# Second expert layer as seven block products with a transposed output

## The chip, the cores and the metric

The kernel runs on one core of a Trainium2 chip. Its engines run side by side, each with a queue of its own that is worked off in order: TensorE (PE; its weight loads are shown as PEld), VectorE (DVE), ScalarE (ACT), GpSimd (POOL) and SyncE (SP), which issues transfers. The metric is device time in microseconds (us) for one execution; the time before is the median of three runs.

## The reference

A block of a transformer on x of 8 x 1024 tokens with 256 numbers each, all in float32. First comes attention with 16 heads, rotary positions and a residual. Then a mixture of 8 experts: each expert takes the 1024 tokens with the highest gate score out of all 8192, and adds its gated output to their rows.

```
xf = layernorm(x).reshape(8192, 256)
scores = softmax(xf @ gate_w.T)             # 8192 x 8 experts
vals, idx = top_k(scores.T, 1024)           # per expert: 1024 tokens
y = layernorm(xf[idx]) * ln_w + ln_b        # 1024 x 256 for each expert
h = gelu(y @ fc1.T + b1)                    # 1024 x 1024
out = (h @ fc2.T + b2) * vals               # 1024 x 256
xf = xf.at[idx].add(out)
```

## The kernel before

The attention stage fills roughly the first 1680 us of the profiled execution. After it, a search by bits finds each expert's threshold, and from about 1747 us on the experts follow one another. The change lies in this expert stage alone.

The work of one expert e has these parts:

- **Token list** (`token_list`, built in pieces by `list_piece`): VectorE compares, TensorE sums small products (L1142) into `ps_i`, and VectorE writes the list `idx` of 1024 rows. It is worked on piece by piece, one or two experts ahead.
- **Gather** (`gather`): eight indirect transfers on GpSimd's queue (L1179), 128 rows each, fetch tokens and gates into two tiles `g`.
- **Turned rows** (`turned_rows`): 8 transposes on TensorE for each half (L1194) and two operations on VectorE (L1195) give `yT`, with the 256 dimensions on the partitions and 512 tokens along the row.
- **First layer**: expert 0 is computed plainly (`first_layer`, L1238). Experts 1 to 7 use a 2x2 block form with 7 block products instead of 8 (`first_layer_by_seven`, L1279): the blocks are the two halves of 256 dimensions, of 1024 hidden units and of 1024 tokens. Sums of weight blocks are made by GpSimd (`weight_sums`, L1257 to L1260), sums of token blocks by VectorE (`row_sums`, L1266 to L1269). For each f of 0 to 3, seven matmuls of 128x512 write seven PSUM banks from the pool `ps_h` (5 banks). ScalarE copies the first product (L1291), VectorE recombines (L1295 to L1324), and ScalarE applies gelu with the bias (L1231), giving `hT`: hidden units on the partitions, tokens along the row.
- **Second layer** (`second_layer`, L1333): for each of 8 tiles of 128 tokens, 8 matmuls of 128x256 with `hT` as the stationary operand give a tile with tokens on the partitions. VectorE adds the bias (L1341) and multiplies by the gate, one number per partition (L1342). GpSimd scatters the tile into `out` with an adding indirect transfer (L1343). These scatters write the same tensor, and each waits until the one before has landed.

The order of all engines' work is the order in which the program is written (`manual_schedule`): nothing is reordered. The loop over experts writes the first layer of e, then its second layer tile by tile, and between the tiles the preparation of expert e+1 (gathers before tiles 0 and 1, `weight_sums` before tile 2, turned rows before tiles 4 and 5) and a piece of list e+2 before each tile. The last expert, 7, splits its first layer in a part "a" before the second layer and a part "b" between its tiles.

Each profiled matmul of the program appears as two records in float32, so a second-layer tile shows 16 records. A transpose appears as one.

## Time and profile before

| | |
|---|---|
| runs before | 2210.72, 2214.38, 2216.36 us; median 2214.38 |
| profiled execution | 2207.54 us, span 2205.8 us |
| busy over the span | PE 93%, DVE 80%, ACT 63%, POOL 58% |
| granted TensorE clock, mean | 0.978 |
| expert 1, first layer, from | 1812.7 us |
| last token scatter issued at | 2200.31 us |

"Busy" is the time in which an engine works on something; an engine can hold its queue without being busy, while its next instruction waits. The tables by line give an operation's count and mean time. Start times count from the start of the span. The chain of waits follows the work that ended last back in time and names the engine whose work it was at each moment.

### The profile page before, as it was taken

Reading aid. Unit: us, or ns where it says so; the run is one execution under the profiler, and the core shown is the slowest. Engines: PE = TensorE matmul, PEld = TensorE weight load, DVE = VectorE, ACT = ScalarE, POOL = GpSimd, SP = SyncE. Lnnn points to the kernel's source line nnn. Section 1 sums busy time; section 2 is a strip of 40 time slices with the busy share of each in tenths; the row PEclk is TensorE's granted clock in tenths of the full one; section 3 lists DMA queues with packets and bytes.
Section 4 is the critical chain, followed back from the end, with each engine's and each line's share of the span. In section 5 each row is a group of like instructions: output and inputs, shape, how many; then the busy total and the mean of one; then the engine's idle time right before and its main releaser. Section 6 shows DMA issues by size and latency. Waiting matters only on the chain.

```text
span 2205.8 us, 35134 instructions
## 1 busy us (share of the span) xinstructions
PE 2056.1 (93%) x12528; PEld 1100.0 (50%) x12528; DVE 1765.4 (80%) x3446; ACT 1384.7 (63%) x1791; POOL 1272.5 (58%) x1320
## 2 busy tenths in 40 slices
PE   7999999999999999999999999999993599999998
PEld 4444544444444444444444444444431376666665
DVE  8988888998998899889989988989946646666654
ACT  2777777777887777878777877877781112222222
POOL 6667585848485766758584867644242144444442
PEclk9999999999999999999999999999996699999999
DMA  6523624632372356236323722552114033333322
GB/s 178 191 88 123 238 81 147 223 122 78 136 257 73 104 202 206 96 107 225 143 78 143 270 67 102 188 208 88 41 41 135 20 75 75 77 77 77 76 42 24
DMA packets 152703, 271.53 MB, mean 123 GB/s; under 512 B 15056, under 2 KB 67664, under 8 KB 152400
## 3 DMA queue, kind: packets, MB, share of 16 engines
q1 hardware_dynamic: 139088, 250.62, 32.9%
q0 software_dynamic: 12288, 17.05, 4.7%
q8 instruction: 99, 1.62, 0.3%
q10 hardware_dynamic: 1152, 1.62, 0.2%
q14 instruction: 76, 0.62, 0.1%
HBM read 143.93 MB, written 125.04 MB: 122 GB/s over the span
## 4 chain that ended last, share of the span: by engine, by line
PE 71%; DVE 16%; issue 4%; POOL 3%; ACT 2%; DMA 2%; POOLq 0%; ACTq 0%; SPq 0%; DVEq 0%
PE ps_av L639 20%; DVE mx L543 14%; PE ps_x L536 13%; PE ps_o L1333 10%; PE ps L1279 8%; PE ps_s L587 7%; PE ps_p L292 5%; PE ps_t L251 3%; PE ps_o L727 3%; PE ps_h L1238 1%; POOL xf L242 1%; ACT e L620 1%; PE ps_d L665 1%; DVE xr L735 1%; PE ps_y L1194 1%
## 5 line engine op out<-in xcount | busy, mean ns | idle before, releaser
L543 DVE TENSOR_REDUCE mx<-ps_x 128x1 f32<-128x512 f32 x2048 | 1264.1, 681 | 153.1 <-PE ps_x L536 139.8
L620 ACT ACTIVATE e<-ps_s 128x1024 f32<-128x1024 f32 x1024 | 995.4, 1025 | 88.6 <-PE ps_x L536 42.1
L536 PE MATMUL ps_x<-k,q 64*128 64x512 f32 x2048 | 718.9, 449 | 19.7 <-DVE mx L543 6.2
L587 PE MATMUL ps_s<-q,s 64*128 64x512 f32 x2048 | 622.2, 428 | 9.0 <-ACT e L620 6.1
L536 PEld LDWEIGHTS ps_x<-k,q 64*128 64x128 f32 x2048 | 347.4, 185 | 414.1 <-DVE mx L543 287.8
L639 PE MATMUL ps_av<-e,v 128*32 128x512 f32 x4096 | 492.5, 598 | 6.9 <-DVE mx L543 0.9
L654 POOL TENSOR_TENSOR av<-av,avp 128x512 f32<-128x512 f32 x190 | 242.4, 1276 | 396.4 <-ACT avp L652 380.2
L587 PEld LDWEIGHTS ps_s<-q,s 64*128 64x128 f32 x2048 | 314.0, 185 | 46.9 <-ACT e L620 29.6
L1333 PE MATMUL ps_o<-w,hT 128*128 128x256 f32 x1024 | 230.2, 381 | 0.0
L639 PEld LDWEIGHTS ps_av<-e,v 128*32 128x32 f32 x4096 | 107.0, 109 | 241.7 <-issue 163.6
L1343 POOL DMA_INDIRECT out<-o,idx x64 | 103.0, 1609 | 212.9 <-DVE o L1342 80.2
L1333 PEld LDWEIGHTS ps_o<-w,hT 128*128 128x128 f32 x1024 | 191.8, 190 | 29.3 <-issue 4.8
L652 ACT COPY avp<-ps_av 128x512 f32<-128x512 f32 x192 | 112.8, 587 | 144.4 <-PE ps_av L639 139.9
L1231 ACT ACTIVATE hT<-mid,b 128x512 f32<-128x512 f32 x112 | 77.9, 719 | 98.9 <-DVE mid L1306 73.9
L1291 ACT COPY mid<-ps 128x512 f32<-128x512 f32 x28 | 16.0, 571 | 195.7 <-PE ps L1279 195.7
L292 PE MATMUL ps_p<-wqkv,xnT 128*128 128x512 f32 (+1 forms) x288 | 129.8, 578 | 4.5 <-DVE mx L543 4.1
L1341 DVE TENSOR_TENSOR o<-ps_o,b2b 128x256 f32<-128x256 f32 x64 | 27.1, 423 | 128.8 <-PE ps_o L1333 126.2
L269 POOL TENSOR_TENSOR u<-pe,sin 128x256 f32<-128x256 f32 (+1 forms) x128 | 86.2, 695 | 53.8 <-ACT pe L263 53.8
L1179 POOL DMA_INDIRECT g<-rows_d,idx x64 | 63.9, 998 | 92.1 <-issue 68.0
L339 POOL CAST hi<-full 128x512 fp32r<-128x512 f32 x60 | 36.9, 615 | 89.8 <-ACT full L337 80.7
L273 POOL TENSOR_TENSOR qk<-pe,u 128x512 f32<-128x512 f32 (+1 forms) x72 | 83.3, 1157 | 7.2 <-DVE pe L271 2.2
L340 POOL TENSOR_TENSOR lo<-full,hi 128x512 fp32r<-128x512 f32 x60 | 76.9, 1281 | 7.5 <-DMA s_d<-dlo 2.9
(200 smaller groups left out, 2323.8 us busy)
## 6 DMA issues: line engine op xcount, KB each, us to landing
s<-s_d SPq DMA_DIRECT2D x64, 512.0 KB
k<-k_d SPq DMA_DIRECT2D x62, 512.0 KB
q<-q_d SPq DMA_DIRECT2D x124, 256.0 KB
s_d<-dhi SPq DMA_DIRECT2D x32, 512.0 KB
s_d<-dlo SPq DMA_DIRECT2D x32, 512.0 KB
w<-in_fc_t SPq DMA_DIRECT2D x16, 1024.0 KB
q_d<-hi SPq DMA_DIRECT2D x30, 512.0 KB
q_d<-lo SPq DMA_DIRECT2D x30, 512.0 KB
```

What stands on the lines that cost most here:

```text
L269: eng.tensor_tensor(u[:, :, a * hd : (a + 1) * hd], v4[:, :, 1 - a, :], s3, ALU.mult)
L292: nc.tensor.matmul(pp, lhsT=xnT[:, kc, t % T2 * P : (t % T2 + 1) * P], rhs=w.rearrange("p a d -> p (a d)") if n == DC else w, start=(kc == 0),
L536: nc.tensor.matmul(pt, lhsT=q[r : r + 64, h // 2, j * P : (j + 1) * P], rhs=k[r : r + 64, h // 2, kh * QW : (kh + 1) * QW], start=True, st ...
L543: nc.vector.tensor_reduce(grp[i]["mx"][:, kh, h, j : j + 1], pt, AX.X, ALU.max)
L587: nc.tensor.matmul(pt[:, h % 2, :], lhsT=ones_r[r : r + 64, :] if last else k[r : r + 64, pair, kt * P : (kt + 1) * P], rhs=(top_bufs[half ...
L620: nc.scalar.activation(e.rearrange("p h q -> p (h q)"), pt.rearrange("p h q -> p (h q)"), AF.Exp, scale=DH**-0.5,)
L639: nc.tensor.matmul(pa[HS * h : HS * (h + 1), :], lhsT=v_bufs[b % 2][:, kt, c : c + HS], rhs=es[h // 2][:, h % 2, :], start=(n == 0), stop= ...
L652: nc.scalar.copy(part, pa)
L654: (nc.vector if end else nc.gpsimd).tensor_tensor(av, av, part, ALU.add)
L1279: nc.tensor.matmul(ph, lhsT=lhsT, rhs=rhs, start=True, stop=True)
L1333: nc.tensor.matmul(po, lhsT=h[:, f, j * P : (j + 1) * P], rhs=weights[e][1][:, f, :], start=(n == 0), stop=(n == FC - 1),)
L1343: nc.gpsimd.indirect_dma_start(out=out_rows[:, :], out_offset=bass.IndirectOffsetOnAxis(ap=idx[:, t : t + 1], axis=0), in_=o, in_offset=No ...
```

## The change

For experts 1 to 6 the second layer also becomes a 2x2 block form with 7 block products. The blocks are the two halves of the 256 output dimensions, of the 1024 hidden units and of the 1024 tokens.

- The weights become the stationary operand and the hidden values, 128x512, the moving one. Each product is 4 matmuls of 128x512 into one bank of `ps_h`. The output comes out transposed: dimensions on the partitions, tokens along the row.
- GpSimd makes four sums of second-weight blocks (`second_weight_sums`), written at the start of expert e.
- VectorE makes four sums of hidden blocks for each f (`sum_hidden`), written behind the first layer of f+1. One of them overwrites a block of `hT`.
- VectorE recombines the products; the bias enters with ScalarE's copy of the first product and with one VectorE operation. For this the bias is loaded a second time with output dimensions on the partitions (`b2t`).
- The recombined blocks are turned back by TensorE, 2 transposes for each tile of 128 tokens (`leave`), into the two banks of `ps_o`. ScalarE multiplies by the gate while copying out, and GpSimd scatters as before.
- The first half of the tokens leaves after six products, before the last one. The second half leaves in the next expert, after its first-layer step f=0 (`later`).
- The preparation of e+1 and the list pieces are placed by `between`, called twice in each product (slots 0 to 13). Three slots hold no list piece, so 11 do.
- To make room, `hT` has 2 buffers instead of 3, the buffers `mid2` and `mid3` 2 instead of 4, some list tiles one fewer; `o` has 7 instead of 4.

Experts 0 and 7 keep the second layer as it was, and the attention stage is untouched.

```diff
--- before.py
+++ after.py
@@ -986,6 +986,12 @@
     )
 
 
+    b2t = sel.tile([P, E, 2], F32, name="b2t")
+    with nc.allow_non_contiguous_dma("16 numbers per partition"):
+        nc.scalar.dma_start(b2t, b2.rearrange("e (i p) -> p e i", p=P))
+    nc.gpsimd.tensor_tensor(b2t[:, :, 1], b2t[:, :, 1], b2t[:, :, 0], ALU.subtract)
+
+
     lane_i = sel.tile([P, P], I32, name="lane_i")
     nc.gpsimd.iota(lane_i, pattern=[[1, P]], base=0, channel_multiplier=0)
     lane = sel.tile([P, P], BF16, name="lane")
@@ -1104,7 +1110,7 @@
         n_odd, HIGH, CH = P // LOW, K // LOW, 1024 // LOW
         order = turn if n_odd == 2 else lane[:, 0:HIGH]
         mine = by_token[:, e].rearrange("p b t -> p (b t)")
-        halves_i = hot.tile([P, 2, NT], I32, tag="halves_i", name=f"halves_i{e}")
+        halves_i = hot.tile([P, 2, NT], I32, tag="halves_i", name=f"halves_i{e}", bufs=1)
         nc.vector.tensor_scalar(halves_i[:, 0], mine, LOW - 1, None, ALU.bitwise_and)
         nc.vector.tensor_scalar(halves_i[:, 1], mine, LOW.bit_length() - 1, None, ALU.logical_shift_right)
 
@@ -1124,12 +1130,12 @@
             two = numbers.rearrange("p (l a) -> p l a", a=2).unsqueeze(1)
             return two.to_broadcast([P, tiles, two.shape[2], 2])
 
-        high = hot.tile([P, NT, HIGH], BF16, tag=f"high{LOW}", name=f"high_{e}")
+        high = hot.tile([P, NT, HIGH], BF16, tag=f"high{LOW}", name=f"high_{e}", bufs=3 - n_odd)
         nc.vector.tensor_tensor(
             in_pairs(high), each(split[:, 1], HIGH), rows_of(order, NT), ALU.is_equal
         )
         yield
-        ids = hot.tile([P, NT, 2, HIGH], BF16, tag=f"ids{LOW}", name=f"ids_{e}")
+        ids = hot.tile([P, NT, 2, HIGH], BF16, tag=f"ids{LOW}", name=f"ids_{e}", bufs=3 - n_odd)
         nc.vector.tensor_scalar(ids[:, :, 0, :], high, part, None, ALU.mult)
         nc.vector.tensor_tensor(
             in_pairs(ids[:, :, 1, :]), in_pairs(high), each(lane2, HIGH), ALU.mult
@@ -1151,7 +1157,7 @@
         lows = []
         for c in range(NT // CH):
             yield
-            low = hot.tile([P, 1024], BF16, tag="low", name=f"low_{e}_{c}", bufs=4)
+            low = hot.tile([P, 1024], BF16, tag="low", name=f"low_{e}_{c}", bufs=3)
             low = low.rearrange("p (c l) -> p c l", l=LOW)
             nc.vector.tensor_tensor(
                 in_pairs(low),
@@ -1225,7 +1231,7 @@
             )
 
     def hidden(e, half):
-        return act.tile([P, FC, 512], F32, tag="hT", name=f"hT_{e}_{half}", bufs=3)
+        return act.tile([P, FC, 512], F32, tag="hT", name=f"hT_{e}_{half}", bufs=2)
 
     def activated(e, f, h, src, cols=slice(0, 512)):
         nc.scalar.activation(
@@ -1248,7 +1254,7 @@
 
 
     FH = FC // 2
-    MIDS = {1: 2, 2: FH, 3: FH, 4: 2, 5: 2}
+    MIDS = {1: 2, 2: 2, 3: 2, 4: 2, 5: 2}
 
     def weight_sums(e):
         w = weights[e][0]
@@ -1291,11 +1297,11 @@
             nc.scalar.copy(m1, p1)
             p6 = bank(6)
             product(p6, s[:, 1, lo], t[:, 1])
-            u2 = mid(2)
+            u2 = mid(2) if e + 1 < E else hidden_sum(e, 0)[:, f]
             nc.vector.tensor_tensor(u2, p6, m1, ALU.add)
             p7 = bank(7)
             product(p7, s[:, 2, lo], t[:, 2])
-            u3 = mid(3)
+            u3 = mid(3) if e + 1 < E else hidden_sum(e, 1)[:, f]
             nc.vector.tensor_tensor(u3, p7, u2, ALU.add)
             kept[e, f] = u2, u3
         if "b" in part:
@@ -1324,6 +1330,98 @@
             nc.vector.tensor_tensor(c12, p3, u2, ALU.add)
             activated(e, f, hs[1], c12)
 
+
+
+    def hidden_sum(e, i):
+
+        if (e, i) not in hidden_sums:
+            hidden_sums[e, i] = one.tile([P, FH, 512], F32, tag=f"hsum{i}", name=f"hsum{i}_{e}")
+        return hidden_sums[e, i]
+
+    def sum_hidden(e, f, hs):
+
+        t1, t2, t4 = (hidden_sum(e, i)[:, f] for i in range(3))
+        lo, hi = f, FH + f
+        nc.vector.tensor_tensor(t1, hs[1][:, lo], hs[0][:, lo], ALU.subtract)
+        nc.vector.tensor_tensor(t2, hs[1][:, hi], t1, ALU.subtract)
+        nc.vector.tensor_tensor(t4, hs[0][:, hi], t2, ALU.subtract)
+        nc.vector.tensor_tensor(hs[1][:, lo], hs[1][:, hi], hs[1][:, lo], ALU.subtract)
+
+    def second_weight_sums(e):
+        w = weights[e][1]
+        a = [[w[:, k * FH : (k + 1) * FH, i * P : (i + 1) * P] for k in range(2)] for i in range(2)]
+        s = one.tile([P, 4, FH, P], F32, tag="w2sum", name=f"w2sum_{e}")
+        nc.gpsimd.tensor_tensor(s[:, 0], a[1][0], a[1][1], ALU.add)
+        nc.gpsimd.tensor_tensor(s[:, 1], s[:, 0], a[0][0], ALU.subtract)
+        nc.gpsimd.tensor_tensor(s[:, 2], a[0][0], a[1][0], ALU.subtract)
+        nc.gpsimd.tensor_tensor(s[:, 3], a[0][1], s[:, 1], ALU.subtract)
+        sums2[e] = s
+
+    def second_layer_by_seven(e, hs, between):
+
+
+        w, s = weights[e][1], sums2[e]
+        t1, t2, t4 = (hidden_sum(e, i) for i in range(3))
+        lo, hi = slice(0, FH), slice(FH, FC)
+        mid = lambda i: act.tile([P, 512], F32, tag=f"mid{i}", name=f"mid{i}", bufs=MIDS[i])
+        slot = [0]
+
+        def product(i, a, b):
+            pt = ps_h.tile([P, 512], F32, tag="ph", name=f"ps_{i}")
+            for c in range(FH):
+                if c % 2 == 0:
+                    between(slot[0])
+                    slot[0] += 1
+                nc.tensor.matmul(
+                    pt, lhsT=a[:, c, :], rhs=b[:, c, :], start=(c == 0), stop=(c == FH - 1)
+                )
+            return pt
+
+        def leave(half, parts):
+
+            g = gathered[e, half]
+            for j in range(4):
+                po = ps_o.tile([P, D], F32, tag="po", name="ps_o")
+                for i, part in enumerate(parts):
+                    nc.tensor.transpose(
+                        po[:, i * P : (i + 1) * P], part[:, j * P : (j + 1) * P], ident
+                    )
+                o = act.tile([P, D], F32, tag="o", name="o", bufs=7)
+                nc.scalar.mul(o, po, g[:, j, D + e : D + e + 1])
+                add_to_out(e, 4 * half + j, o)
+
+        p1 = product(1, w[:, lo, 0:P], hs[0][:, lo])
+        m1 = mid(1)
+        nc.scalar.activation(m1, p1, AF.Identity, bias=b2t[:, e, 0:1])
+        p2 = product(2, w[:, hi, 0:P], hs[0][:, hi])
+        c11 = mid(5)
+        nc.vector.tensor_tensor(c11, p2, m1, ALU.add)
+        p6 = product(6, s[:, 1], t2)
+        u2 = mid(2)
+        nc.vector.tensor_tensor(u2, p6, m1, ALU.add)
+        p7 = product(7, s[:, 2], hs[1][:, lo])
+        u3 = mid(3)
+        nc.vector.scalar_tensor_tensor(u3, p7, b2t[:, e, 1:2], u2, ALU.add, ALU.add)
+        p4 = product(4, w[:, hi, P:D], t4)
+        c21 = mid(4)
+        nc.vector.tensor_tensor(c21, p4, u3, ALU.add)
+        p5 = product(5, s[:, 0], t1)
+        nc.vector.tensor_tensor(u2, p5, u2, ALU.add)
+        nc.vector.tensor_tensor(u3, p5, u3, ALU.add)
+        leave(0, (c11, c21))
+        p3 = product(3, s[:, 3], hs[1][:, hi])
+        nc.vector.tensor_tensor(u2, p3, u2, ALU.add)
+        return lambda: leave(1, (u2, u3))
+
+    def add_to_out(e, t, o):
+        nc.gpsimd.indirect_dma_start(
+            out=out_rows[:, :],
+            out_offset=bass.IndirectOffsetOnAxis(ap=lists[e][:, t : t + 1], axis=0),
+            in_=o,
+            in_offset=None,
+            compute_op=ALU.add,
+        )
+
     def second_layer(e, half, j, h):
         idx, t, g = lists[e], 4 * half + j, gathered[e, half]
         po = ps_o.tile([P, D], F32, tag="po", name="ps_o")
@@ -1337,19 +1435,14 @@
                 start=(n == 0),
                 stop=(n == FC - 1),
             )
-        o = act.tile([P, D], F32, tag="o", name="o", bufs=4)
+        o = act.tile([P, D], F32, tag="o", name="o", bufs=7)
         nc.vector.tensor_tensor(o, po, b2b[:, e, :], ALU.add)
         nc.vector.tensor_scalar(o, o, g[:, j, D + e : D + e + 1], None, ALU.mult)
-        nc.gpsimd.indirect_dma_start(
-            out=out_rows[:, :],
-            out_offset=bass.IndirectOffsetOnAxis(ap=idx[:, t : t + 1], axis=0),
-            in_=o,
-            in_offset=None,
-            compute_op=ALU.add,
-        )
+        add_to_out(e, t, o)
 
     assert KT == 8 and FC == 2 * FH
     lists, gathered, turned, sums, row_sum, kept = {}, {}, {}, {}, {}, {}
+    hidden_sums, sums2 = {}, {}
     places(0, 1)
     keep_busy(10)
     for _ in token_list(0, P // 2, 0):
@@ -1402,33 +1495,44 @@
             if half == 1 and j == 3:
                 row_sums(1)
             second_layer(0, half, j, h)
+    later = None
     for e in range(1, E):
         if e + 1 < E:
             load_weights(e + 1)
+            second_weight_sums(e)
         hs = [hidden(e, half) for half in range(2)]
         for f in range(FH):
             first_layer_by_seven(e, f, hs, "ab" if e + 1 < E else "a")
+            if later is not None:
+                later()
+                later = None
             list_piece(1, e + 1)
+            if e + 1 < E and f > 0:
+                sum_hidden(e, f - 1, hs)
         if e + 1 < E:
+            sum_hidden(e, FH - 1, hs)
             list_piece(99, e + 1)
-        for t in range(KT):
-            if e + 1 < E:
-                if t < 2:
-                    gather(e + 1, t)
-                if t == 2:
+
+            def between(i):
+                if i in (0, 2):
+                    gather(e + 1, (i - 0) // 2)
+                if i == 5:
                     weight_sums(e + 1)
-            list_piece(1, e + 2)
-            if e + 1 < E:
-                if t in (4, 5):
-                    turned_rows(e + 1, int(t == 5))
-                if t == 5:
+                if i >= 3:
+                    list_piece(1, e + 2)
+                if i in (9, 11):
+                    turned_rows(e + 1, int(i == 11))
+                if i == 12:
                     row_sums(e + 1)
-            second_layer(e, t // 4, t % 4, hs[t // 4])
-
-
-            if e + 1 == E and t < FH:
-                first_layer_by_seven(e, t, hs, "b")
-
+
+            later = second_layer_by_seven(e, hs, between)
+        else:
+
+
+            for t in range(KT):
+                second_layer(e, t // 4, t % 4, hs[t // 4])
+                if t < FH:
+                    first_layer_by_seven(e, t, hs, "b")
 
 # ---- launch: one core; numpy only lays the arrays out ----
 def _rotary_tables(n, d):
```

## Prediction

> **What bounds the kernel now.** I read the page's slices first, then busy time by stage, then the chain of waits over the expert stage, then the queues of VectorE, ScalarE and GpSimd in order of time. The slices show that TensorE fills the expert stage; by stage, one steady expert (55.6 us) looks like this (columns: window, length, busy PE, PEld, DVE, ACT, POOL, granted clock, DMA share, GB/s):
>
> ```profile
> PE   7999999999999999999999999999993599999998
> 1923.00:1978.60 55.60, 55.60 (x266) 38.16 (x265) 36.82 (x68) 13.11 (x20) 26.40 (x20) 1.00 0.35 77
> ```
>
> PE is busy 55.6 of 55.6 us at clock 1.00. The chain of waits (start, length, work) runs through PE alone: first layer (L1279), second layer (L1333), turned rows (L1194), pieces of token list (L1142). At the very end it leaves PE for the scatters into out:
>
> ```profile
> 1923.02 6.01 PE ps L1279 x14
> 1947.92 10.36 PE ps_o L1333 x48
> 1974.89 0.19 PE ps_i L1142 x8
> 1975.08 3.56 PE ps_o L1333 x16
> 2128.57 0.87 PE ps_y L1194 x8
> 2191.14 3.86 DMA out<-o,idx
> ```
>
> GpSimd is "busy" for 26.4 us only, but its queue stands far longer: each scatter waits until the one before has landed. ScalarE's three activations and VectorE's sums give the other prices:
>
> ```profile
> 2191.14 1.54 POOL L1343 DMA_INDIRECT out<-o,idx  x1 [3.03 <-DMA out<-o,idx]
> 2195.75 1.54 POOL L1343 DMA_INDIRECT out<-o,idx  x1 [3.07 <-DMA out<-o,idx]
> 2200.31 1.54 POOL L1343 DMA_INDIRECT out<-o,idx  x1 [3.02 <-DMA out<-o,idx]
> 1961.01 1.85 POOL L1257 TENSOR_TENSOR wsum<-w 128x512 f32<-128x512 f32 x1
> 1964.72 1.26 POOL L1259 TENSOR_TENSOR wsum<-w 128x512 f32<-128x512 f32 x1
> 1928.47 2.04 ACT L1231 ACTIVATE hT<-mid,b 128x512 f32<-128x512 f32 x3 [0.54 <-DVE mid L1313]
> 1969.45 0.68 DVE L1266 TENSOR_TENSOR ysum<-yT,yT 128x512 f32<-128x512 f32 x1
> 1970.16 0.69 DVE L1267 TENSOR_TENSOR ysum<-yT,ysum 128x512 f32<-128x512 f32 x1
> 1970.77 0.69 DVE L1268 TENSOR_TENSOR ysum<-yT 128x512 f32<-128x512 f32 x1
> ```
>
> Scatters that follow each other stand 4.56 to 4.61 us apart here (4.46 to 4.68 elsewhere). VectorE's operations start 0.71 us apart where one needs the last, 0.60 otherwise.
>
> **Matmuls.** I call F the start of an expert's first layer, S the start of its second, p1 to p7 its products in the order p1, p2, p6, p7, p4, p5, p3. Removed: 8 tiles x 3.455 us (10.36 / 3) = 27.64. Added: 28 matmuls of 128x512; the first layer has the same shape at 6.01 / 7 = 0.858 us, so 24.02. Added: 16 turns of 128x128; eight turned rows take 0.87, so 1.74. A change of work costs the next group 0.10 (3.56 against 3.455), twice: 0.20. Sum 25.96, so PE saves 1.68 us per expert if nothing waits. The list pieces and turned rows are the same number as before.
>
> The Trainium skill ("TensorE: Matmul & The Clock Gate", Part 4: PE-mode transpose) gives about 275 ns for a 128x128 turn inside a kernel, which speaks against this change: 16 would be an estimated 4.4 us and the saving would be a loss of 1.0. The trace's mean for one is 276 ns as well, but eight in a row advance the chain by 0.87, which is what I use.
>
> **New wait 1: turning back the second half.** It is issued after f=0 of the next expert. Two output tiles are free; the third pair of turns waits until ScalarE has scaled the first. In ScalarE's queue that scaling stands behind f=0's four activations, the last of which ends at F+7.49 (1928.47 + 2.04 - 1923.02). The scaling of 128x256 out of PSUM is not in the trace: below it a copy of 128x128 (0.27) and above it an activation of 128x256 (0.47); a copy of 128x512 is 0.59. I take 0.42. So pair three starts at F+7.97, pair four 0.36 later, the pairs take 0.22, and f=1 starts at F+8.55 instead of 6.01 + 0.87: 1.67 us lost (1.4 to 1.9), with all of f=1 queued behind and VectorE idle too. The first half is turned with ScalarE free: the same wait costs 1.37 against 0.87, so 0.50 (0.4 to 0.6).
>
> **VectorE.** Removed per expert: 8 x (0.42 + 0.35) of bias and gate. Added: 16 sums of hidden blocks and 7 recombinations. In the recorded order the list pieces leave the first layer, the hidden sums enter it. For f=1 on (clock from its start): 7 operations need 0.71 x 2 + 0.60 x 5 = 4.42, four sums 0.71 x 2 + 0.60 x 2 = 2.62, together 7.04 against 6.01 on PE. Sums of f=0 run from 6.65, f=2 from 9.27, its sums from 13.69, f=3 from 16.31, the last sums until 25.97, that is S+7.95. Five PSUM banks just cover it: f=3's last product starts at 17.17 and needs a bank that is read by 17.00. Products p1 and p2 cover the sums that p6 needs. But the new list's first piece comes after: 7.95 + 1.07 (four small ones, 1948.57 to 1949.64) + 0.60 + 0.66 + 0.68 = S+10.96, and PE wants it at S+10.3: 0.70 lost (0 to 2.0, since 0.25 us more or less per step moves it by that).
>
> **Sums of second weights on GpSimd.** Four operations, 5.1 to 7.4 us by the rows 1.26 and 1.85. They have one buffer that p3 of the expert before reads last, and four scatters stand ahead, so they run at about S+41 to S+47 of that expert: F+11 to 17 of the next, well ahead of their reader at S+6.9. They hide, but their end lies beside VectorE's first hidden sums. The slow rows 1.85 and 1.81 are those beside VectorE's work on SBUF, so I add 0.5 us of lag per expert (0 to 2.5: four operations held one each).
>
> The skill ("SBUF — State Buffer", Who interferes with whom) says a VectorE operation with two SBUF inputs and a GpSimd one that reads SBUF exclude each other. By that all overlap would be paid, an estimated 1 to 2 us per expert; the rows show only 0.5 to 0.6 per operation.
>
> **GpSimd's queue.** Per period: two runs of four scatters at 3 x 4.57 + 1.54 = 15.25, weight sums 6.2 twice, gathers 8 x 1.27 = 10.2: 53.1 us, under the period. Gathers then start at about S+5.5 rather than S-5, land by S+18.6, and PE turns their second half at S+21.7: hidden, 3 us to spare.
>
> **The end.** For the last changed expert (6; no list pieces) S6 was 2114.76 and the last scatter issued at 2200.31, S6+85.55. Scatters used to leave from S+4 on; now the first waits for six products: 20.6 + 1.82 of turned rows + 0.74 for turn and scaling = S6+23.2. Sixteen scatters then stand in line (8 of this expert, 8 of the last), and those of the last expert would be ready from S6+52, before their turn at 59.8. So the last one issues at 23.2 + 15 x 4.57 = S6+91.75: 6.2 us later (4.5 at 4.46, 7.9 at 4.68). TensorE ends near S6+82, so it no longer matters there.
>
> **At nothing.** Buffers cut from 3 or 4 to 2 or 3: their last readers (p3; a list piece two slots back) are done when they are written. The new load of biases in 4-byte pieces stands last in ScalarE's DMA queue (after 1690.8); behind its wait on GpSimd is the mask that PE reads at 1727.0, a cover of 36 us while the threshold search runs. Such a load is not in the trace; a small one (4 KB) lands in 3.0 us here, and even ten times that is covered; beyond the cover each microsecond would count. Moved weight loads only get earlier.
>
> **Sum.** Per period -1.68 + 1.67 + 0.50 + 0.70 + 0.50 = +1.69. From S1 to S6 there are five periods: +8.45. With the end: +14.65. The profiled execution took 2207.54 (span 2205.8), so 2222.2; the median of the runs is 6.84 above that execution, so I say 2229.
>
> **Rivals.**
> 1. TensorE stays the only limit: faster. No wait costs anything, five periods give -8.4, the end another -1.6: 2204. For it: PE is 100% busy now. Against: the scatters. Even with no stall at all the line of sixteen gives -8.4 + 6.2; a gain above 0.3% (6.6 us, what a measurement here can tell from none) needs spacing below 4.28, and no row has that. 6%.
> 2. Little change (within 6.6 us): PE's waits mostly vanish because scaling is short and VectorE keeps up; -2 to +6, so 2212 to 2221. Against: ScalarE's order fixes wait 1. 16%.
> 3. VectorE and GpSimd become the bound of the first layer: each exclusion is paid and PSUM banks run out, +4 per period, 20 + 6.2: 2241. For it: 7.04 against 6.01, and a bank margin of 0.17. 18%.
> 4. The forecast, waits as summed: 60%.
>
> Low ends together give 5 x 0.12 + 4.5 = +5, high ends 5 x 5.3 + 7.9 = +34, both unlikely. I take 2214 to 2243, into rivals 2 and 3. Faster 0.06, same 0.16, slower 0.78.
>
> **What would show it.** Right: second-layer products at 0.86 us a matmul; a gap on PE of about 1.7 us after f=0, released by ScalarE; a period near 57.3; sixteen scatters in line at the end, about 4.57 apart, with PE done some 10 us before. Wrong: a period at or under 55.6, no PE gap at the turns, or a last scatter released by VectorE's output rather than by the scatter before it.

## The result and the profile after

The changed kernel takes 2237.57 us (median of 4 runs, 2232.74 to 2238.29), the kernel before, run beside it, 2214.93: a ratio of 1.0107, 95% interval 1.0095 to 1.0119. It is slower by 22.6 us. The forecast was 2229, +14.65 in its sum: the right side and mostly the right places, with most of them priced too low and one wait, for PSUM banks, put at nothing.

The profiled execution took 2237.21 us (span 2235.2). 5.40 us of its distance to the one before lie ahead of expert 1 (it starts at 1817.89 instead of 1812.49), 5.20 of them ahead of the threshold search (its first product on PE starts at 1689.54 instead of 1684.34), in work that the change doesn't touch. So I compare the expert stage: from the first product of expert 1 to the issue of the last scatter it was 2200.31 - 1812.49 = 387.82 us, and is 2229.59 - 1817.89 = 411.70, or +23.88, within 1.3 us of the medians.

One steady expert and the page's slice row of PE (columns as in the prediction: window, length, busy PE, PEld, DVE, ACT, POOL, clock, DMA share, GB/s):

```profile
PE   7998999999999999999999999999971899999996
1934.54:1992.47 57.93, 55.08 (x209) 25.81 (x208) 46.64 (x75) 16.99 (x29) 31.96 (x24) 1.00 0.34 73
```

PE was busy for all of its 55.6 us; now it is busy for 55.08 of 57.93. VectorE went from 36.8 to 46.6. Where PE's time goes is seen in its queue in order of time (start, length, line, tile, and in brackets the idle time before with its releaser; `...` stands for rows of work without a gap):

```profile
1940.55 0.60 PE L1386 MATMUL ps_o<-ident,mid 128*128 128x128 f32 x4
1942.61 0.80 PE L1386 MATMUL ps_o<-ident,mid 128*128 128x128 f32 x4 [1.46 <-ACT o L1390]
1943.25 1.02 PE L1285 MATMUL ps<-yT,w 128*128 128x512 f32 x2
...
1960.92 1.13 PE L1285 MATMUL ps<-yT,wsum 128*128 128x512 f32 x2 [0.34 <-DVE mid L1301]
...
1973.16 0.36 PE L1148 MATMUL ps_i<-ids,low 128*128 128x16 bf16 x8 [0.70 <-DVE low L1162]
...
1986.88 0.60 PE L1386 MATMUL ps_o<-ident,mid 128*128 128x128 f32 x4
1987.83 0.80 PE L1386 MATMUL ps_o<-ident,mid 128*128 128x128 f32 x4 [0.35 <-ACT o L1390]
1988.47 0.35 PE L1148 MATMUL ps_i<-ids,low 128*128 128x16 bf16 x8
```

Four stalls. The second half's turns take 2.70 us from start to f=1 (1940.55 to 1943.25) where eight without a wait take 0.87: 1.83 lost, to ScalarE. The last product of f=3 waits for a PSUM bank that VectorE has not read, and S comes 0.61 late by it (1961.89, where 1955.27 and the 6.01 us of an f give 1961.28). The new list comes 0.87 late, from VectorE. The first half's turns take 1.59: 0.72 lost. Together that is 4.03 of the 57.93 us.

ScalarE's queue shows why the first is so long: the scaling (L1390) stands behind three gelus:

```profile
1940.09 2.10 ACT L1237 ACTIVATE hT<-mid,b 128x512 f32<-128x512 f32 x3 [0.41 <-DVE mid L1319]
1942.10 0.82 ACT L1390 ACTIVATE o<-ps_o,g 128x256 f32<-128x256 f32 x2
```

Expert 1 is worse. From the start of its second layer, S1, to that of expert 2, S2, it is 61.55 us; the next three steps are 57.94, 57.92 and 58.84, the last 57.72. VectorE's hidden sums and GpSimd's sums of the next first weights stand beside each other there (queues of VectorE and GpSimd):

```profile
1845.29 1.76 DVE L1345 TENSOR_TENSOR hsum<-hT,hT 128x512 f32<-128x512 f32 x1
1847.08 1.64 DVE L1346 TENSOR_TENSOR hsum<-hT,hsum 128x512 f32<-128x512 f32 x1
1845.23 1.27 POOL L1265 TENSOR_TENSOR wsum<-w 128x512 f32<-128x512 f32 x1
1846.45 1.72 POOL L1266 TENSOR_TENSOR wsum<-w,wsum 128x512 f32<-128x512 f32 x1
```

A hidden sum takes 0.68 to 0.69 where no sum of GpSimd runs beside it. The list then comes 2.58 us late, and after that gap the granted clock falls, so that the next two groups of four records take 3.10 and 2.43 us instead of 1.96 (PE's queue, then the window with the clock in the third column from the end):

```profile
1855.56 0.36 PE L1148 MATMUL ps_i<-ids,low 128*128 128x16 bf16 x8 [2.58 <-DVE low L1162]
1855.77 3.10 PE L1375 MATMUL ps<-hT,w2sum 128*128 128x512 f32 x4
```

```profile
1856.00:1859.00 3.00, 3.00 (x13) 1.06 (x12) 1.30 (x3) 0.00 (x0) 0.00 (x0) 0.58 0.00 0
```

At the end sixteen scatters stand in line, the last ones released by the scatter before (GpSimd's queue). PE is done at 2218.4, 11 us before the last of them is issued:

```profile
2160.01 1.62 POOL L1417 DMA_INDIRECT out<-o,idx  x1 [3.77 <-ACT o L1390]
2166.00 1.57 POOL L1417 DMA_INDIRECT out<-o,idx  x1 [4.37 <-ACT mid L1297]
...
2229.59 1.55 POOL L1417 DMA_INDIRECT out<-o,idx  x1 [3.00 <-DMA out<-o,idx]
```

The first leaves at S6 + 23.64 (S6 is 2136.37), and fifteen gaps of 4.64 on average follow (the first is 5.99, the other fourteen are 4.54 on average).

### The profile page after: what moved, and what is told of

It is laid out like the page before. It is cut to its first block, busy times and chain, and to the rows that moved or that the text cites. A ratio compares the mean times of both kernels' runs of the same rounds, so it can differ in the third digit from the quotient of the medians.

```text
span 2235.2 us, 34636 instructions
## 1 busy us (share of the span) xinstructions
PE 2058.6 (92%) x12192; PEld 1027.6 (46%) x12192; DVE 1829.8 (82%) x3488; ACT 1408.4 (63%) x1845; POOL 1306.6 (58%) x1345
## 5 line engine op out<-in xcount | busy, mean ns | idle before, releaser
L1390 ACT ACTIVATE o<-ps_o,g 128x256 f32<-128x256 f32 x48 | 20.3, 469 | 128.7 <-PE ps_o L1386 128.7
L339 POOL CAST hi<-full 128x512 fp32r<-128x512 f32 x60 | 36.8, 613 | 88.7 <-ACT full L337 81.4
L271 POOL TENSOR_TENSOR pe<-pe,cos 128x512 f32<-128x512 f32 (+1 forms) x64 | 77.5, 1210 | 5.0
L1285 PE MATMUL ps<-ysum,wsum 128*128 128x512 f32 x168 | 77.4, 593 | 0.2 <-DVE mid L1314 0.2
L263 ACT COPY pe<-ps_p 128x512 f32<-128x512 f32 (+1 forms) x64 | 35.9, 561 | 61.9 <-PE ps_p L292 61.9
```

Source lines behind the costliest of these rows:

```text
L1285: nc.tensor.matmul(ph, lhsT=lhsT, rhs=rhs, start=True, stop=True)
```

## The experiments

Each kernel was timed in five rounds against the kernel before. The first column of numbers is the difference to before by medians of one call (the change itself: +22.6), the second the ratio and its interval, the third the expert stage by the trace of one execution, against the 411.70 of the change. The experiments are variants of the changed kernel, and their edits are given against it or against the variant named.

| kernel | us | ratio | stage |
|---|---|---|---|
| k1_banks | +42.9 | 1.0201 (1.0182 to 1.0220) | +12.0 |
| k2_ahead | +15.6 | 1.0075 (1.0059 to 1.0091) | -6.4 |
| k3_wsum | +25.2 | 1.0105 (1.0087 to 1.0124) | +0.5 |
| k4_plain6 | +13.9 | 1.0064 (1.0048 to 1.0079) | -8.5 |
| k6_turnfirst | +23.6 | 1.0113 (1.0097 to 1.0128) | -0.6 |
| k7_nosum | +22.0 | 1.0108 (1.0093 to 1.0123) | -3.6 |
| k8_all | +9.4 | 1.0038 (1.0024 to 1.0052) | -17.6 |
| k9_late | +20.3 | 1.0088 (1.0069 to 1.0108) | -4.1 |
| k10_late_turn | +14.8 | 1.0064 (1.0043 to 1.0085) | -6.6 |
| k11_all | +9.7 | 1.0043 (1.0029 to 1.0058) | -15.8 |
| k12_gather | -1.4 | 0.9994 (0.9985 to 1.0002) | -23.8 |
| k13_apart | -8.8 | 0.9960 (0.9946 to 0.9973) | -32.1 |

The kernel before stands at -23.9 in the last column.

**k1_banks.** Two tiles in each bank of `ps_o`:

```diff
             for j in range(4):
-                po = ps_o.tile([P, D], F32, tag="po", name="ps_o")
+                if j % 2 == 0:
+                    both = ps_o.tile([P, 2, D], F32, tag="po", name="ps_o")
+                po = both[:, j % 2]
```

> The four output tiles that one half turns back share two full PSUM banks (two 128x256 tiles in each), so no turn waits for a scaling of ScalarE. Theory (each period loses what the trace of the changed kernel shows at the turns: 1.84 us in the second half, 0.72 in the first, both released by ScalarE): five periods of 2.56 us give -12.8 us, about 2225; groups of turns advance the chain by 0.87 each, the wait of PE for o is gone, and the first scatter of expert 6 starts some 0.5 us earlier. Rival A (the first layer is held by VectorE and GpSimd anyway, as the prediction's rival 3 has it): VectorE has less time before f=1 and falls behind, the stall comes back as a wait for PSUM banks or for the list, and no more than 1 us per period is won: -5 or less. Rival B: the end's line of scatters sets the time and what PE gains before it is lost there: no change.

A miss: the edit made the wait it was to remove longer, since now each second turn waits for the scaling of the other tile in its bank (PE's queue, steady expert):

```profile
1939.50 0.38 PE L1388 MATMUL ps_o<-ident,mid 128*128 128x128 f32 x2
1941.56 0.66 PE L1388 MATMUL ps_o<-ident,mid 128*128 128x128 f32 x4 [1.68 <-ACT o L1392]
1942.93 0.44 PE L1388 MATMUL ps_o<-ident,mid 128*128 128x128 f32 x2 [0.71 <-ACT o L1392]
```

The turns take 3.70 us instead of 2.70, those of the first half 2.59 instead of 1.59. It still answers something: 2.0 us more of wait made the steady period 1.6 longer (59.5 against 57.9), so a wait at the turns does lie on the path. The later periods are longer still, 60.8 to 61.3. The profiled run was the shortest of five (2245.87 to 2261.86), with a mean granted clock of 0.976; the others lost 9 to 16 us more at 0.969 to 0.972, and where, the trace of this one can't show.

**k2_ahead.** List pieces consumed two pieces later:

```diff
-            yield from token_list(e, P)
+            yield from token_list(e, P, 2)
```

> TensorE consumes each piece of the token list two pieces later instead of one. Theory: PE's wait for the list right after the second layer's first products is 0.9 to 0.95 us in a steady period and 2.6 in expert 1, where the granted clock then falls to 0.58 and costs about 1.9 more; without it 4 x 0.93 + 4.5 = 8 us are won, about 2230, and the clock stays at 1.00 through expert 1. Rival: the list is only where VectorE's lag shows, and its next late result (the mid that p6 or p7 needs) holds PE by as much: no more than 2 us are won.

As the theory had it, with 6.4 of its 8 us. The list wait is gone except for 0.87 us in expert 1, where the clock stays at 1.00; steady periods are 56.8 instead of 57.93.

**k3_wsum and k7_nosum.** The same question, asked twice: first with GpSimd's sums of first weights three slots later, then with the four sums for expert 2 left out, which uses those of expert 1 instead:

```diff
-                if i == 5:
+                if i == 8:
                     weight_sums(e + 1)
```

> The sums of the next expert's first weights on GpSimd are issued three slots later in the second layer (slot 8 instead of 5). Theory: in expert 1 alone they run beside VectorE's last hidden sums (1.76 and 1.64 us instead of 0.68), and moved they leave those at 0.68: VectorE is free some 2 us earlier in expert 1, its list wait shrinks from 2.6 to below 1, the clock does not fall there, and about 3.5 us are won (2234); other experts keep their times within 0.3 us. Rival (the slow hidden sums come from something else, such as the scatter's reads or PE's): the same two sums still take 1.6 us or more and the time is the same within 1 us.

Nothing moved. In GpSimd's queue no other instruction stands between the two slots, so the sums started 0.24 us after the second layer, as before (1846.62 for S1 at 1846.38). The run says nothing on the cause; the second one does:

```diff
-                if i == 5:
+                if i == 5 and e == 1:
+                    sums[2] = sums[1]
+                elif i == 5:
                     weight_sums(e + 1)
```

> Leaves out of the computation the four sums of expert 2's first weights on GpSimd (expert 2 uses those of expert 1); everything else stays. k3_wsum had not moved these sums on GpSimd (nothing stands in its queue between the two slots; they started 0.24 us after the second layer in both). Theory (a VectorE operation on two SBUF operands and a GpSimd one exclude each other): expert 1's two hidden sums of 1.76 and 1.64 us go to 0.68, its list wait shrinks from 2.6 to below 1 us, the granted clock stays at 1.00 there, and 3 to 4 us are won in expert 1 alone, 2234. Rival (they are slow for another reason): no change, within 1 us.

With GpSimd silent, expert 1's last hidden sums take 0.68 and 0.69 (VectorE's queue, the sums that took 1.76 and 1.64), its list wait 0.55 (PE's queue), and the clock is 1.00:

```profile
1843.45 0.68 DVE L1345 TENSOR_TENSOR hsum<-hT,hT 128x512 f32<-128x512 f32 x1
1844.16 0.69 DVE L1346 TENSOR_TENSOR hsum<-hT,hsum 128x512 f32<-128x512 f32 x1
1851.69 0.36 PE L1148 MATMUL ps_i<-ids,low 128*128 128x16 bf16 x8 [0.55 <-DVE low L1162]
```

That is 3.6 us less in the stage, all of it between F1 and F2, the starts of the first layers of experts 1 and 2 (54.88 for 58.57). The medians (-0.6 against the change) are too coarse for it; the trace is the evidence.

**k4_plain6.** Expert 6 with the second layer of the kernel before.

```diff
-            later = second_layer_by_seven(e, hs, between)
+            if e < 6:
+                later = second_layer_by_seven(e, hs, between)
+            else:
+                for t in range(KT):
...
+                    second_layer(e, t // 4, t % 4, hs[t // 4])
```

> Expert 6 alone keeps the plain second layer, with its scatters leaving from the first tile on; experts 1 to 5 are as in the change. Theory (the end is the line of sixteen scatters that starts late): from expert 6's second layer to the last scatter 85.5 us instead of 93.1, that is -7.5 us, about 2230, though TensorE itself does 1.7 us more work there and ends with the scatters. Rival (the end is held by PE's and VectorE's work of the last expert, and the scatters only follow): slower by about 1 to 2 us, since PE has more to do.

Right: 8.5 us in the stage. The last scatters but three are released by VectorE's tile again, 5.17 apart, and only the last three by the scatter before.

**k6_turnfirst.** k1_banks mended: both tiles of a bank are turned, then both are scaled.

```diff
-            for j in range(4):
-                po = ps_o.tile([P, D], F32, tag="po", name="ps_o")
+            for j0 in (0, 2):
+                both = ps_o.tile([P, 2, D], F32, tag="po", name="ps_o")
+                for j in (j0, j0 + 1):
+                    for i, part in enumerate(parts):
+                        nc.tensor.transpose(
...
+                for j in (j0, j0 + 1):
+                    o = act.tile([P, D], F32, tag="o", name="o", bufs=7)
+                    nc.scalar.mul(o, both[:, j - j0], g[:, j, D + e : D + e + 1])
```

> As k1_banks, but both tiles of a bank are turned before either is scaled. k1_banks had each second turn wait for the scaling of its neighbour in the same bank (1.68 and 0.71 us at one half, 0.57 and 0.71 at the other), so that the turns grew by 1.0 us per half instead of shrinking. Theory (a period is as long as what TensorE waits for at the turns, one for one, as long as VectorE is not later than it): now all eight turns of a half follow each other in 0.87 us, 1.84 + 0.72 us per period are won, -12.8 in five, less 0.3 to 0.6 per period if f=3's product waits for a PSUM bank or the list waits longer: -9 to -13, 2225 to 2229. Rival A (VectorE and GpSimd bound the first layer): TensorE's wait only moves to the banks and the list, -5 or less. Rival B (ScalarE's scalings, now later in the queue, hold the next activations and through them the sums): -5 or less, with VectorE's hidden sums waiting for ScalarE's gelus.

The wait that I had counted as the largest is gone, eight turns advance PE by 0.87 (1935.85 to 1936.72), and nothing is won. Rival A holds; rival B doesn't, since VectorE has no gap ahead of its hidden sums and so never waits for a gelu there. PE's waits over the same five periods (engine, line, released by: us in total, times, longest), first of the change, then of k6_turnfirst:

```profile
PE ps_o L1386 <- ACT o L1390: 9.1, 10, 1.5
PE ps_i L1148 <- DVE low L1162: 5.2, 5, 2.6
PE ps L1285 <- DVE mid L1301: 2.1, 6, 0.5
```

```profile
PE ps L1285 <- DVE mid L1301: 10.7, 10, 2.4
PE ps_i L1148 <- DVE low L1162: 5.0, 5, 2.6
PE ps L1285 <- DVE mid L1314: 1.0, 5, 0.2
```

9.1 us of waiting for ScalarE turned into 8.6 more of waiting for VectorE. There are two reasons in VectorE's queue: it needs 7.2 us per f where PE needs 6.0, and because it comes earlier now, its first hidden sums meet GpSimd's sums of second weights. In the change they had come just as the last of these ended (in a steady expert only the first hidden sum was touched, 0.90 for 0.68). The rows are of k6_turnfirst:

```profile
1944.96 1.64 DVE L1346 TENSOR_TENSOR hsum<-hT,hsum 128x512 f32<-128x512 f32 x1
1946.64 1.64 DVE L1347 TENSOR_TENSOR hsum<-hT,hsum 128x512 f32<-128x512 f32 x1
1946.02 1.71 POOL L1357 TENSOR_TENSOR w2sum<-w,w2sum 128x512 f32<-128x512 f32 x1
```

**k8_all.** k6_turnfirst, k2_ahead and k4_plain6 together.

> Turning first (k6_turnfirst), list pieces two ahead (k2_ahead) and a plain second layer for expert 6 (k4_plain6) together. Theory (three separate losses that add up): -10 to -13 for the turns, -8 for the list, -9 for the end, together -27 to -30 against the change: 2208 to 2211, 2 to 5 us below the kernel before. Rival (they share one cause, VectorE's lag, or the queue of GpSimd at 53 us per period takes over): no more than -20, 2217 or above, not faster than the kernel before.

-17.6: 2.1 more than the sum of the single stages (-0.6, -6.4, -8.5), but far short of the theory, which still counted the turns at 10 to 13. 6.8 us of waiting for VectorE in the first layer remain.

**k9_late, k10_late_turn, k11_all.** Two of the four hidden sums leave the first layer; they are made once, four times as wide. k10_late_turn adds the edit of k6_turnfirst, k11_all also those of k2_ahead and k4_plain6:

```diff
         nc.vector.tensor_tensor(t2, hs[1][:, hi], t1, ALU.subtract)
-        nc.vector.tensor_tensor(t4, hs[0][:, hi], t2, ALU.subtract)
-        nc.vector.tensor_tensor(hs[1][:, lo], hs[1][:, hi], hs[1][:, lo], ALU.subtract)
+        if f == FH - 1:
+            t2, t4 = hidden_sum(e, 1), hidden_sum(e, 2)
+            lo, hi = slice(0, FH), slice(FH, FC)
+            nc.vector.tensor_tensor(hs[1][:, lo], hs[1][:, hi], hs[1][:, lo], ALU.subtract)
+            nc.vector.tensor_tensor(t4, hs[0][:, hi], t2, ALU.subtract)
```

> Two of the four hidden sums (t4 and the one of p7) leave the first layer: they are made once, 2048 wide, after the last narrow one. VectorE then has some 5.8 us of work per f in the first layer instead of 7.0, against 6.0 of TensorE. In k6_turnfirst the turns no longer waited for ScalarE, but TensorE then waited for VectorE in the first layer (10.7 us in five periods, 2.1 in the change), so that nothing was won. Theory (waits for ScalarE and for VectorE stand in for each other; VectorE's queue in the first layer is the next limit): alone this edit wins only the 0.4 us per period that TensorE waits for a bank, -1 to -4 in all, since the wait at the turns stays. Rival (VectorE's queue is the limit by itself, the wait at the turns hides behind it): -8 or more.

> The hidden sums moved as in k9_late, together with turning first as in k6_turnfirst. Theory (they stand in for each other): k6_turnfirst alone won 0 to 1 us and k9_late alone little, both together win the 1.84 + 0.72 us at the turns and the bank wait in each of five periods: -10 to -15 against the change, periods near 55. Rival (another wait comes next, for the list or for GpSimd's queue of 53 us per period): -5 or less.

> The hidden sums moved, turning first, list pieces two ahead and a plain second layer for expert 6. k8_all, which has all but the hidden sums, is still 6 us longer than the kernel before in the expert stage, with 6.8 us of TensorE's waits for VectorE in the first layer. Theory: those go, periods of 54 to 55 us, 2 to 8 us faster than the kernel before (ratio 0.996 to 0.999). Rival (GpSimd's queue, or VectorE's sums beside GpSimd's, take over): no faster than the kernel before.

k9_late: -4.1, the bank wait gone, as the theory had it; its list wait in expert 1 grew from 2.58 to 3.88. k10_late_turn won 6.6 of the 10 to 15: the rival's part is in its list wait, which grew from 5.2 to 11.4 us in five periods: PE comes earlier, and the wide sums stand before the list. k11_all has the list two ahead, and so should have been free; it is no better than k8_all. PE's waits name the next one:

```profile
PE ps_y L1200 <- DMA g<-rows_d,idx: 8.6, 6, 2.3
```

The gathered rows are late. On GpSimd's queue the gathers stand behind eight scatters and a set of sums, and were issued at S+11 to S+20.

**k12_gather.** k11_all with the second half's scatters held back until the gathers are issued; only expert 1 still gathers between its products:

```diff
+            if f == 0 and e > 1:
+                for half in range(2):
+                    if e + 1 < E:
+                        gather(e + 1, half)
+                for one_of in held:
+                    add_to_out(*one_of)
```

> As k11_all, but the eight gathers of the next expert's rows stand ahead of the second half's four scatters in GpSimd's queue, from expert 2 on, and the sums of first weights behind these scatters. In k11_all TensorE no longer waits for ScalarE and hardly for VectorE, but 8.6 us for gathered rows: the gathers stood behind eight scatters and two sets of sums and were issued at S+11 to S+20. Theory (GpSimd's queue is the limit that came next, by its order and not by its length of 53 us): the wait for gathered rows goes, periods of 54 to 55 us, 5 to 10 us off k11_all, ratio to the kernel before 0.997 to 1.000. Rival (the length is the limit: sixteen things in a row per period take 53 to 57 us whatever their order, and the first sums or the scatters at the end come late instead): within 3 us of k11_all, ratio 1.003 to 1.005.

8 us less than k11_all in the stage, level with the kernel before, with periods of 54.4 to 54.7 after expert 1's. The order of GpSimd's queue was the limit, not its length. Two places remained: 2.26 us of list wait in expert 1, and in expert 6 VectorE's row sums at 1.64 to 2.67 us each beside GpSimd's sums, with 2.50 us of PE behind them.

**k13_apart.** k12_gather with GpSimd's sums moved off both places:

```diff
+                if i == 6 and e == 1:
+                    after = it.tile([P, 1], F32, tag="after", name="after")
+                    nc.gpsimd.tensor_copy(after, kept["u2"][:, 0:1])
-                if i == 5:
+                if i == (6 if e == 1 else 5):
                     weight_sums(e + 1)
...
-                    if t == 2:
+                    if t == 0:
                         weight_sums(e + 1)
```

> As k12_gather, with GpSimd's sums of first weights moved away from VectorE's operations on two SBUF operands at the two places where they still stood beside them: for expert 2 behind the third recombination of expert 1 (a 128x1 copy of its result holds them), for expert 7 ahead of expert 6's scatters. In k12_gather expert 1's last hidden sums took 1.64 to 1.75 us each instead of 0.68 and TensorE waited 2.26 us for the list behind them; expert 6's four row sums took 1.64 to 2.67 and TensorE waited 2.50 for an output tile and then ran 16 products in 5.41 us instead of 3.6. Theory (the two exclude each other, so the order alone brings the time back): both groups at 0.68 to 0.9, TensorE's waits gone, -2 in expert 1 and -4 in expert 6: ratio to the kernel before 0.996 to 0.998, faster than it. Rival (the sums find another neighbour in their new place, the list pieces in expert 1 and the gating in expert 6, or the scatters behind them are late at the end): within 2 us of k12_gather.

Faster than the kernel before by 0.4%: 0.9960 (0.9946 to 0.9973), -8.8 us. The hidden sums in expert 1 take 0.68 to 0.69, the row sums in expert 6 the same, and PE has one wait of 0.2 us left in the whole stage. The rival was right that the sums find another neighbour, but PE doesn't wait for it: in expert 1 two list comparisons now take 2.96 us together instead of 1.28 (the row below; in the change's steady expert a pair already took 2.81), in expert 6 one multiplication by the gate 1.51 instead of 0.35. The window is a steady expert:

```profile
1856.39 2.96 DVE L1162 TENSOR_TENSOR low<-split,lane 128x1024 bf16<-128x1024 bf16 x2
```

```profile
1923.85:1977.65 53.80, 53.80 (x210) 26.23 (x209) 47.08 (x69) 16.47 (x29) 34.45 (x24) 1.00 0.37 79
```

## Why the prediction was right in sign and short in size

The step from sum to time first: adding 6.84 us to the profiled execution is the same as putting the sum on the median of the runs before, 2214.38 + 14.65 = 2229.0. On the 2214.93 measured beside the change it is 2229.6, hardly another number. What was short is the sum, 14.65 for 23.88. Starts are those of PE's queue, so S6 before is 2114.60, where the prediction took 2114.76 from the chain:

| term | forecast | measured |
|---|---|---|
| matmuls, per period | -1.68 | 57.93 less the four waits of 4.03 is 53.90: -1.70 (k13_apart, with no wait: 53.80) |
| new wait 1 | +1.67 | +1.83 |
| first half turned | +0.50 | +0.72 |
| PSUM banks in the first layer | 0, "just cover it" | +0.61 |
| list piece | +0.70 | +0.87 |
| exclusion, per period | +0.50 | steady 0.2 on VectorE, within the two rows above; +3.6 in expert 1; about +0.9 in the period that ends at S5 |
| expert 1's first layer, ahead of S1 | not counted | +0.47, a wait for a bank |
| period | 57.3 | 57.93 steady, 58.8 mean |
| end | +6.2 | +7.5 |

**Matmuls.** Right, and shown by the version with no waits. Turns at 0.87 for eight were the right price: k6_turnfirst shows it for the very turns. The Trainium skill's figure ("TensorE: Matmul & The Clock Gate", Part 4: PE-mode transpose) of 275 ns for one, which I weighed against it, does not add up for turns in a row here.

**Waits.** Both waits at the turns were right in place and releaser, and 0.16 and 0.22 short, mainly because scaling costs 0.47 us and not 0.42: the upper of the two bounds was the right one. VectorE is free at S+8.2 (forecast 7.95), and the list 0.17 later than forecast (its own terms, 10.96 less 10.3, give 0.66 and not 0.70).

**The banks** are the first step that failed: a margin of 0.17 us, put at no cost, was negative. VectorE needs 7.24 us per f (1952.95 to 1960.19), not 7.04, and so lags more with each f. Most of the difference is in the seven recombinations, 4.58 for 4.42: where one needs the last, they start 0.78 to 0.80 apart and not 0.71, a distance read from the row sums. VectorE's queue before had it:

```profile
1943.73 0.69 DVE L1295 TENSOR_TENSOR mid<-ps,mid 128x512 f32<-128x512 f32 x1 [1.11 <-PE ps L1279]
1944.53 0.69 DVE L1299 TENSOR_TENSOR mid<-ps,mid 128x512 f32<-128x512 f32 x1
```

With 0.61 in a steady period and 0.47 ahead of S1, the banks make up about 3.5 of the 9.2 us by which the sum was short. In a steady period the three small errors (0.55 together) and the 0.61, less the 0.50 for exclusion and 0.02 on the matmuls, are the 0.64 by which it is longer than forecast.

**Exclusion** is the other step that failed. I read its price from GpSimd's rows 1.85 and 1.81 and spread 0.5 over every expert. The row of 1.85 is no sign of it: the first of the four sums takes 1.83 to 1.86 in every expert whenever a scatter stands just before it, and 1.27 or 1.28 where none does (1842.65). VectorE's rows show the price: a hidden sum of 0.68 becomes 1.64 to 1.80, about 1.0 to 1.1 more, where a sum of GpSimd takes 1.27 alone. And PE pays for it only where the two queues meet at a place that it waits for, most in expert 1, where GpSimd has no scatters ahead and so runs early, with a set of sums that I had not considered (those of the first weights). In the two periods where PE paid it cost 4.5 us, for 2.5 forecast over five. The Trainium skill ("SBUF — State Buffer", Who interferes with whom) says that a VectorE instruction with two SBUF inputs contends with a GpSimd one that reads SBUF, for ports that are locked exclusively; the sums of k7_nosum and k13_apart, 0.68 against 1.64 to 1.80, agree with that, and my reading of the rows as something milder was wrong. The recombinations, with one input in PSUM, kept 0.68 beside GpSimd's sums (1842.89 to 1844.68 in expert 1).

**The end.** Mechanism and place right: the first scatter at S6+23.6 (23.2), sixteen in line, PE done long before. Of the 1.3 us short, 0.44 are the start and 1.0 the spacing, 4.64 and not 4.57, less the 0.16 by which S6 before was taken late. One gap of 5.99 counts for all of the spacing; what made it longer, no run shows. k4_plain6 removes the late line.

**At nothing.** The load of biases was hidden, though slower than any small load seen before: GpSimd waited 12.29 us for it, until 1707.1; the mask behind it is ready at 1709, and PE uses it at about 1732. The gathers began at S+7.3 (forecast S+5.5), and PE did not wait for them.

**The rivals.** The third was nearer than its 18% said: with wait 1 taken away, VectorE and GpSimd are the bound of the first layer (k6_turnfirst). I had added wait 1 and VectorE's lag as if they were independent. For the sum that did little harm, since VectorE idles in the wait and its lag was worked out from f=1 on, but whoever had removed the wait on the strength of this sum would have won nothing. The first rival's -8.4 was no fiction either: it is about what the stage of k13_apart shows against before (379.62 for 387.82), with the waits out of the way and expert 6 plain. The measured 2237.57 lies nearer to the third rival's 2241 than to 2229: the range held because it reached into that rival, while in the change itself the waits for ScalarE, the list and the scatters stood as the forecast had them.

## What to carry to other kernels

When a bound engine is relieved by 3%, price the queues of the others in the same period: here ScalarE, VectorE, GpSimd's gathers and the line of scatters became the limit one after the other, and several waits that were removed laid open the next. Waits in a row on one path stand in for each other, so a wait's length is not what its removal wins; remove it and look who releases the engine next. Where TensorE waits behind it, an operation on two SBUF operands on VectorE should be ordered apart from one on GpSimd, and where GpSimd's queue is long, what others wait for (gathers) goes ahead of what nobody waits for (scatters).

## What the runs showed of the hardware

- TensorE's granted clock stayed at 1.00 after single gaps of 2.26 us (k12_gather, expert 1), 2.27 (k11_all, expert 1) and 2.39 (k6_turnfirst, at 2065.81). It fell to 0.50 after one of 2.10 (k8_all, at 2059.36), to 0.57 after one of 2.30 (k11_all, at 1974.55), to 0.55 after one of 2.50 (k12_gather, expert 6) and to 0.58 after one of 2.58 (the change). So between 2.1 and 2.4 us the length of a gap alone did not decide. In k1_banks it fell to 0.50 once after two gaps of 1.68 and 0.71 within 4 us, and not at the same gaps an expert earlier. The Trainium skill ("TensorE: Matmul & The Clock Gate", What's actually happening) speaks of an idle window of about 3.4 us that runs freely; gaps shorter than that sufficed here, while the freedom of the window would fit the cases that came and went. No run here tests that.
- Two tiles in one PSUM bank made TensorE wait for ScalarE's reading of the other one when their work was written alternately (k1_banks: 0.57 to 0.71 us where ScalarE was free, 1.68 behind its gelus). Whether the chip or the program's own waits ask for it is not told apart by these runs.
- A load of 2048 pieces of 4 bytes held its reader on GpSimd for 12.29 us; it was issued at 1695.95 and the reader ran at 1707.12.
